# Four column modes per mixing matmul, one save of row modes on ScalarE's queue, way back in two tiles, 15 buffers at once

## The chip, the cores and the metric

The kernel runs on one core of one Trainium2 chip. The metric is the device time of one execution in microseconds (us), from repeated runs; lower is better. Beside it stands one execution that the hardware profiler recorded, with every instruction of the five engines (TensorE, called PE, with its weight loads as PEld; VectorE, DVE; ScalarE, ACT; GpSimd, POOL; SyncE, SP) and every DMA packet.

## What is computed

Two layers on one image x of 512 x 512 positions with 64 channels, all in float32.

```
x  = x + L0(group_norm(x))        # gated products of rows, masked; an output gate
x1 = x
out = x1 + L1(group_norm(x1))
L1: X   = fft2(x1_normed)[:12, :12]              # 12 x 12 modes for each channel
    Y   = einsum("comn,cmn->omn", w_real + 1j*w_imag, X)   # mixes channels, mode by mode
    out = real(ifft2(Y placed at [:12, :12]))
```

The change touches only the second layer, L1, and the end of the first. The group norm is affine for each channel, so its scale enters L1 as a factor on the modes and its shift only in mode (0, 0). The kernel therefore collects modes of x1 while x1 is still being made, and applies the norm afterwards.

## The kernel before, in words

The case with few masked rows (`compact`) is the one that runs. The image is handled in 16 column tiles jc of 32 columns, each in four blocks b of 128 rows; one such tile of 128 rows x 32 columns x 64 channels is 1 MB.

**Main loop (lines 1120 to 1230).** 32 units (half a column tile each, 2 MB) follow one another, each in 8 steps n. The order is written out by hand: each engine takes its instructions in the order of the program (`manual_schedule`). A unit's gate goes PE (L979), DVE (L1194, L1200), ScalarE's sigmoid (L1145), POOL's product and sum (L1038, L1042); the finished x1 is stored by SP to the two halves of a DRAM tensor x1_h (`store`, L1058), and DVE takes group-norm statistics of it (L1096). For each tile, PE collects the row modes in PSUM (`transform`, L1069) and `save` (L1075 to L1090) copies them to SBUF on ScalarE (L1077) and writes them by four DMAs of 48 KB to DRAM, `modes_d`, in runs of 256 bytes. Each group of 128 columns is read back by `fetch` (L904) and turned to column modes by PE (`columns`, L896). The last group has 96 columns, tiles 12 to 14; its fetch is issued by ScalarE, at step 5 of the last unit (L1224). Tile 14 is "the last tile but one", `jc == NJ - 2`. Tile 15's modes do not go through DRAM: they are multiplied at L1083 with a basis that ScalarE prepares at steps 2 to 5 of the last unit (`prepare`, L912, 24 activations).

The mixing weights w_real and w_imag (2.3 MB each) are loaded by SP, two DMAs of 64 partitions x 36 KB, at step 3 of the last unit but one (L1230).

**Between the loops (L1234 to L1287).** POOL clears `picks`. The statistics are joined to the affine `ab2` (`group_norm_affine`, L251 to L277; the matmul L1254 stands inside it). DVE writes the scaled modes to `picks` (L1265): for each row mode m and column mode n a block of 128 x 32 that is zero but for two columns. The mixing (L1275) is 144 matmuls, one for each (m, n): 32 columns of `picks` are stationary, and the 64 columns `wide[:, :, m * MODES + n]` of the weights stream past; twelve of them add up in PSUM for each m, and four m at a time use the four column groups of the array. DVE copies the result to `mixed` (L1284).

**Way back.** `back_columns` is called four times, for 128 columns each, the first time before the last loop: 8 matmuls (L1303), copies to `q` (L1312 on DVE for half of the first call, L1314 on ScalarE for the rest), 16 transposes (L1319), and copies to `parts`, which lies where the weights lay (L1322, L1324).

**Last loop (L1332 to L1356).** For each of the 64 tiles: four matmuls (L1340), four DVE additions to the tile of x1 (L1347), a store of 1 MB by SP (L1348). The tiles of x1 are gathered by rows with indirect DMAs on POOL (`fetch_rows`, L923; the DMA's own line is L629), into a ring of AHEAD = 15 buffers. Buffers 13 and 14 lie in `picks`, so their gathers come after the mixing (L1279).

Of the kernel before, what the change touches and what calls it, by code (L numbers as in the profile page):

```python
# [17 lines left out]
P = 128  # L18
N = 512
C = 64  # L20
# [26 lines left out]
def conv_preact_kernel(ctx: ExitStack, tc: tile.TileContext, t: dict):  # L47
# [565 lines left out]
    def compact(fc):  # L613
# [193 lines left out]
        with tc.tile_pool(name="tri", bufs=1) as trp:  # L807
# [57 lines left out]
            with tc.manual_schedule(), tc.tile_pool(name="late", bufs=1) as lp:  # L865
# [65 lines left out]
                with tc.tile_pool(name="np_x", bufs=LEAD + 2) as tp, tc.tile_pool(  # L931
# [143 lines left out]
                    def save(jc):  # L1075
                        ft = places[:, 7 * 64 * C + M2 * C : 7 * 64 * C + 32 * C].rearrange("p (j c) -> p j c", c=C)
                        nc.scalar.copy(ft.rearrange("p j c -> p (j c)"), fs.pop(jc))  # L1077
                        if jc == NJ - 1:
                            ps = ends[0].rearrange("p m n -> p (m n)")
                            for j in range(8):  # L1080
                                for k in range(2):
                                    e = spread_e[:, j, k].rearrange("p m n -> p (m n)")
                                    nc.tensor.matmul(  # L1083
                                        ps[k * C : (k + 1) * C], ft[:, j, :], e,
                                        start=False, stop=(j == 7), tile_position=(0, k * C),
                                    )
# [33 lines left out]
                    for s in range(-LEAD, total_g + 2 * SIZE):  # L1120
# [110 lines left out]

                with tc.tile_pool(name="lq", bufs=1) as qp, tc.tile_pool(name="lx", bufs=1) as xp:

                    picks = qp.tile([P, MODES, MODES, 32], F32, name="picks")  # L1234
                    fetch_rows(len(fetched))
                    nc.gpsimd.memset(picks, 0.0)
                    buffers += [xp.tile([P, JC, C], F32, name=f"lx_t{i}") for i in range(3)]
                    buffers += [place(i)[:, r * JC : (r + 1) * JC] for i in (0, 1) for r in range(2)]
                    spare = places[:, 7 * 64 * C - 8 * 2 * MODES * M2 : 7 * 64 * C]
                    for spare in (spare, picks.rearrange("p m n k -> p (m n k)")):  # L1240
                        buffers += [spare[:, i * JC * C : (i + 1) * JC * C].rearrange("p (n c) -> p n c", c=C) for i in range(2)]
                    for i in range(len(fetched), AHEAD - 2):
                        fetch_rows(i)
                    rinv = qp.tile([P, 4, P], F32, name="rinv")
                    nc.scalar.dma_start(rinv, t["c_rinv"])
                    col_inv = qp.tile([P, 2, 4, P], F32, name="col_inv")
                    nc.scalar.dma_start(col_inv, t["c_col_inv"])
                    with tc.tile_pool(name="sps", bufs=1, space=PSUM) as sps:

                        turned = sps.tile([P, MODES, M2], F32, name="turned")  # L1250

                        def turn_sums():
                            nc.vector.tensor_add(sums, sums, ends[0])
                            nc.tensor.matmul(  # L1254
                                turned.rearrange("p m n -> p (m n)"), turn, sums.rearrange("p m n -> p (m n)"),
                                start=True, stop=True,
                            )

                        ab2 = group_norm_affine(lp, sets, 8, "x1c", turn_sums)
                        v = qp.tile([P, 2, MODES, MODES], F32, name="v_modes")  # L1260
                        nc.vector.tensor_add(v[:, 0], sums[:, :, :MODES], turned[:, :, MODES:])
                        nc.vector.tensor_sub(v[:, 1], turned[:, :, :MODES], sums[:, :, MODES:])
                        for k in range(2):
                            to = picks.rearrange("p m n k -> p m (n k)")[:, :, 12 * k : 12 * k + 33 * 11 + 1 : 33]
                            nc.vector.tensor_scalar(to, v[:, k], ab2[:, 0:1], None, ALU.mult)  # L1265
                            h = slice(k * C, (k + 1) * C)
                            one = picks[h, 0, 0, 12 * k : 12 * k + 1]
                            nc.vector.scalar_tensor_tensor(one, ab2[h, 1:2], float(N * N), one, ALU.mult, ALU.add)

                        mixed_ps = sps.tile([P, 3, C], F32, name="mixed_ps")  # L1270
                        for m3 in range(3):
                            for n in range(MODES):
                                for g in range(4):
                                    m = 3 * g + m3
                                    nc.tensor.matmul(  # L1275
                                        mixed_ps[32 * g : 32 * g + 32, m3, :], picks[:, m, n, :], wide[:, :, m * MODES + n],
                                        start=(n == 0), stop=(n == MODES - 1), tile_position=(0, 32 * g),
                                    )
# [12 lines left out]
                    q = qp.tile([P, C, 32], F32, name="q_sb")  # L1291
                    nc.vector.memset(q[:, :, M2:], 0.0)

                    def back_columns(jb, pq, pt, first):

                        it = parts[:, jb // 2, : 256 * 16].rearrange("p (j o) -> p j o", o=16)
                        for g2 in range(2):
                            ps = pq.tile([P, 2, 4, 2, C], F32, name="q_ps")[:, :, :3]
                            for part in range(2):
                                for i in range(2):  # L1300
                                    g = 2 * g2 + i
                                    h = slice(32 * g, 32 * g + M2)
                                    nc.tensor.matmul(  # L1303
                                        ps[:, i, :, part, :], col_inv[h, part, jb, :], mixed[h],
                                        start=True, stop=True, tile_position=(32 * g, 0),
                                    )
                            for i in range(2):
                                g = 2 * g2 + i
                                dst = q[:, :, 6 * g : 6 * g + 6].rearrange("p o r -> p r o")
# [5 lines left out]
                        by = q.rearrange("p (o g) r -> p o (g r)", g=4)  # L1315
                        for o4 in range(4):
                            ps = pt.tile([P, 4, P], F32, name="it_ps")
                            for i in range(4):
                                nc.tensor.transpose(ps[:, i, :], by[:, 4 * o4 + i, :], ident)  # L1319
# [48 lines left out]
def _constants():  # L1368
# [19 lines left out]
    for part, rows_ in enumerate(((c.T, -s.T), (s.T, c.T))):  # L1388
# [4 lines left out]
    made = {  # L1393
        "c_last_basis": last_basis.reshape(P, RB, M2),
        "c_last_mask": last_mask,
        "c_col_inv": col_inv.reshape(P, 2, 4, P),
        "c_turn": np.kron([[0, 1], [-1, 0]], np.eye(C)),
        "c_iota": np.tile(np.arange(N), (P, 1)),
# [34 lines left out]
```

## Time and profile before

| | |
|---|---|
| runs of the kernel, median of 3 (lowest to highest) | 1845.44 us (1840.19 to 1845.79) |
| the profiled execution | 1835.84 us |
| its span, first to last instruction | 1834.1 us |
| granted TensorE clock, mean | 0.901 |
| PE, DVE, ACT, POOL busy | 89%, 78%, 52%, 52% |
| DMA, mean over the span | 255 GB/s |
| HBM read, written | 278.05 MB, 187.56 MB |

The profile's page has the busy time of each engine, the span in 40 slices with the granted clock and the DMA rate, the chain of work that ended last, and the costliest groups of instructions. The trace behind it answers further questions: who waited for whom, the chain in order of time, busy time and DMA rate in any stretch, and the DMA packets by queue. q1 is SP's DMA queue, q10 is ScalarE's, q0 POOL's. "issue" is time in which the engine waited for nothing that the profile shows. A name with "q" behind it (ACTq, SPq) is the engine's sequencer.

### The profile page before, as it was taken

What the parts mean: (1) busy time and instruction counts of PE and PEld (TensorE: products, weight loads), DVE (VectorE), ACT (ScalarE), POOL (GpSimd) and SP (SyncE); (2) the same over time, 40 slices, a digit from 0 to 9 for tenths busy, and PEclk for the clock granted to TensorE, in tenths of its full rate; (3) what the DMA queues carried; (4) which work ended last, traced back from release to release, by engine and by line L of the source; (5) the groups of instructions that cost most, each with busy time, mean ns of one, the idle gap of its engine ahead of it and who ended that gap; (6) DMA issues with size and microseconds to landing.
All of it is one profiled execution on the core that took longest, in us unless ns stands there. A gap on an engine that the chain in (4) does not pass through costs nothing.

```text
span 1834.1 us, 33997 instructions
## 1 busy us (share of the span) xinstructions
PE 1628.8 (89%) x11630; PEld 1286.6 (70%) x11630; DVE 1422.9 (78%) x2969; ACT 962.2 (52%) x1694; POOL 947.5 (52%) x709
## 2 busy tenths in 40 slices
PE   6679799999899999999999999999999856998772
PEld 5666666664678778897788888888888734665431
DVE  6989677777455547788999999999999975775442
ACT  3566555554222269976777777777777630111000
POOL 3666211111000007788999999999999881112110
PEclk9989899999899999999999999999999977555555
DMA  6999255556656513577777877776777797999999
GB/s 250 386 385 383 86 138 137 137 137 154 208 178 182 175 34 151 221 241 252 260 247 239 291 261 243 237 266 235 257 261 256 219 297 292 424 427 426 426 427 383
DMA packets 188312, 467.97 MB, mean 255 GB/s; under 512 B 34529, under 2 KB 133857, under 8 KB 147041
## 3 DMA queue, kind: packets, MB, share of 16 engines
q1 hardware_dynamic: 158192, 262.40, 42.5%
q0 software_dynamic: 27712, 201.40, 29.2%
q8 instruction: 95, 1.56, 0.3%
q10 hardware_dynamic: 2224, 1.88, 0.3%
q14 instruction: 89, 0.72, 0.1%
HBM read 278.05 MB, written 187.56 MB: 254 GB/s over the span
## 4 chain that ended last, share of the span: by engine, by line
PE 25%; DVE 18%; DMA 12%; POOL 3%; issue 2%; ACT 2%; SPq 1%; DVEq 0%; ACTq 0%; POOLq 0%
DMA out_x<-places 8%; PE w_ps L979 5%; PE c_ps L979 5%; DVE stats2c L1096 4%; DVE z_t L1194 4%; PE t_ps L969 4%; DVE scratch L1012 4%; PE l_ps L1340 4%; PE y_ps L990 4%; DVE z_t L1200 4%; PE f_ps L1069 2%; DMA modes_d<-places 1%; POOL z_t L1038 1%; POOL places L1042 1%; DMA places<-x_h,dst_i 1%
## 5 line engine op out<-in xcount | busy, mean ns | idle before, releaser
L979 PE MATMUL w_ps<-gate_x,xt_c 128*128 128x128 f32 x2048 | 279.5, 280 | 32.3 <-DVE z_t L1194 30.6
L1042 POOL TENSOR_TENSOR places<-places,z_t 128x1024 f32<-128x1024 f32 x127 | 301.1, 2371 | 8.0
L979 PEld LDWEIGHTS w_ps<-gate_x,xt_c 128*128 128x128 f32 x2048 | 251.0, 193 | 48.0 <-DVE z_t L1194 47.8
L979 PE MATMUL c_ps<-center_x,xt_c 128*128 128x128 f32 x2048 | 276.5, 279 | 1.2 <-ACT xt_c L1008 0.6
L979 PEld LDWEIGHTS c_ps<-center_x,xt_c 128*128 128x128 f32 x2048 | 252.4, 194 | 4.0 <-ACT xt_c L974 2.9
L1096 DVE BATCH_NORM_STATS2 stats2c<-places 128x6 f32<-128x128 f32 x1024 | 220.6, 279 | 12.8 <-POOL places L1042 12.8
L1340 PE MATMUL l_ps<-places,rinv 24*128 24x512 f32 x512 | 204.0, 1106 | 29.3 <-DVE places L1347 18.2
L1012 DVE TENSOR_REDUCE scratch<-sq_c 128x16 f32<-128x1024 f32 x160 | 194.6, 1217 | 27.9 <-ACT sq_c L1007 19.4
L1145 ACT ACTIVATE z_t<-z_t 128x1024 f32<-128x1024 f32 x128 | 135.4, 1059 | 138.0 <-DVE z_t L1200 126.1
L1198 POOL TENSOR_TENSOR z_t<-z_t,bias_row_out 128x1024 f32<-128x1024 f32 x32 | 75.7, 2364 | 245.8 <-DVE z_t L1194 241.7
L969 PE MATMUL t_ps<-c_ident,places 128*128 128x128 f32 x1280 | 198.8, 278 | 1.3 <-DVE places L854 1.3
L1340 PEld LDWEIGHTS l_ps<-places,rinv 24*128 24x128 f32 x512 | 119.4, 298 | 108.6 <-DVE places L1347 57.1
L969 PEld LDWEIGHTS t_ps<-c_ident,places 128*128 128x128 f32 x1280 | 144.4, 141 | 60.3 <-issue 50.9
L974 ACT ACTIVATE xt_c<-t_ps,ab_xc 128x512 f32<-128x512 f32 x256 | 176.2, 688 | 10.3 <-PE t_ps L969 9.3
L1194 DVE TENSOR_TENSOR z_t<-w_ps,rs_n 128x512 f32<-128x512 f32 x256 | 172.1, 672 | 3.0 <-PE w_ps L979 2.9
L1004 ACT ACTIVATE sq_c<-c_ps 128x512 f32<-128x512 f32 x256 | 150.7, 589 | 31.3 <-PE c_ps L979 30.8
L1200 DVE TENSOR_TENSOR z_t<-z_t,scratch 128x1024 f32<-128x1024 f32 x128 | 156.3, 1221 | 10.0 <-ACT rs_n L1018 3.8
L679 DVE BATCH_NORM_STATS2 stats1c<-x_ps 128x6 f32<-128x512 f32 x256 | 156.5, 687 | 8.3 <-PE x_ps L678 7.8
L1038 POOL TENSOR_TENSOR z_t<-z_t,places 128x1024 f32<-128x1024 f32 x64 | 151.6, 2369 | 17.0 <-ACT z_t L1145 13.6
L1347 DVE TENSOR_TENSOR places<-places,l_ps 128x512 f32<-128x512 f32 x176 | 110.2, 684 | 59.3 <-DMA places<-x_h,dst_i 39.8
L1038 POOL TENSOR_TENSOR z_t<-z_t,bias_row_out 128x1024 f32<-128x1024 f32 x63 | 149.3, 2370 | 10.0 <-ACT z_t L1145 9.8
L733 POOL COPY rbc<-rq_out 128x512 f32<-128x512 f32 x64 | 38.3, 613 | 210.5 <-DVE rq_out L209 132.1
(213 smaller groups left out, 2744.3 us busy)
## 6 DMA issues: line engine op xcount, KB each, us to landing
x_h<-places SPq DMA_DIRECT2D x64, 1024.0 KB
out_x<-places SPq DMA_DIRECT2D x44, 1024.0 KB
places<-u_d SPq DMA_DIRECT2D x512, 64.0 KB
left_d<-o_c SPq DMA_DIRECT2D x64, 256.0 KB
right_d<-o_c SPq DMA_DIRECT2D x64, 256.0 KB
left_raw<-left_d SPq DMA_DIRECT2D x64, 256.0 KB
right_raw<-right_d SPq DMA_DIRECT2D x64, 256.0 KB
u_d<-z_t SPq DMA_DIRECT2D x32, 512.0 KB
```

The lines of the kernel that those rows point to most:

```text
L679: nc.vector.bn_stats(stats[:, 0, 16 * (jc % quarter) + 4 * r + c, :], ps.rearrange("p i k -> p (i k)"))
L969: nc.tensor.transpose(tps[:, i, :], flat[:, o : o + P], ident)
L974: nc.scalar.activation(xts[s], tps, AF.Identity, bias=ab1[:, 2:3])
L979: nc.tensor.matmul(ps[:, 2 * i : 2 * i + 2, :], xts[s][:, i, :], w, start=True, stop=True)
L1004: nc.scalar.activation(sq, cps, AF.Square)
L1012: nc.vector.tensor_reduce(totals[k % 2][:, 8 * (n - 1) : 8 * (n + 1)], sqs.pop(s // 2), AX.X, ALU.add)
L1038: nc.gpsimd.tensor_mul(zs[k, c], zs[k, c], u)
L1042: nc.gpsimd.tensor_add(xr, xr, zs.pop((k, c)))
L1096: nc.vector.bn_stats(st[k // 4][:, g, k % 4, :], x_of(k)[:, :, 2 * g : 2 * g + 2])
L1194: nc.vector.tensor_mul(z[:, 8 * odd : 8 * odd + 8, :], wps, rs)
L1200: nc.vector.tensor_add(z, z, bias_ps["ogate"].unsqueeze(1).to_broadcast([P, 16, C]))
L1340: nc.tensor.matmul(ps.rearrange("p j o -> p (j o)"), rinv[h, b, :], it[h], start=True, stop=True, tile_position=(32 * g, 0),)
```

## The change

1. `save` of tile 14 issues its four DMAs to `modes_d` on ScalarE's queue in place of SP's, and the fetch of the last 96 columns is issued at step 4 of the last unit in place of step 5.
2. `picks` holds, for each m, three blocks (q) in place of twelve: a block has the scaled modes of four column modes in four adjacent columns. A matmul of the mixing takes one block against 256 streamed columns (16 x 4 x 4: the 64 channels, reordered, times four n). There are 36 of them, three for each m. Of a row's four sums, one belongs to it: the mask `pick4` (a new constant of 128 x 4, loaded on ScalarE's queue) and a sum over four pick it out. The reordering of the channels that the three copies did is now in the streamed operand. `picks` is a quarter of its size.
3. `q` becomes two tiles of 32 channels. In the first call of `back_columns` DVE copies the first tile and ScalarE the second; in the others ScalarE copies both. The zeros behind them are set by POOL, in place of DVE.
4. The last loop's buffers 4 to 8 are five tiles of a pool (there were three), and none lies in `picks`; all 15 gathers stand before the mixing.

```diff
                         for g in range(4):
                             o = jc * JC + 8 * g
-                            nc.sync.dma_start(modes_d[o : o + 8].rearrange("j m c -> m j c"), ft[32 * g : 32 * g + M2])
+                            queue = nc.scalar if jc == NJ - 2 else nc.sync
+                            queue.dma_start(modes_d[o : o + 8].rearrange("j m c -> m j c"), ft[32 * g : 32 * g + M2])
...
-                        if (v, n) == (last, 5):
+                        if (v, n) == (last, 4):
                             fetch(3)
...
-                    picks = qp.tile([P, MODES, MODES, 32], F32, name="picks")
+                    picks = qp.tile([P, MODES, 3, 32], F32, name="picks")
...
-                    buffers += [xp.tile([P, JC, C], F32, name=f"lx_t{i}") for i in range(3)]
+                    buffers += [xp.tile([P, JC, C], F32, name=f"lx_t{i}") for i in range(5)]
...
-                    for i in range(len(fetched), AHEAD - 2):
+                    for i in range(len(fetched), AHEAD):
                         fetch_rows(i)
+                    pick4 = qp.tile([P, 4], F32, name="pick4")
+                    nc.scalar.dma_start(pick4, t["c_pick4"])
...
                         for k in range(2):
-                            to = picks.rearrange("p m n k -> p m (n k)")[:, :, 12 * k : 12 * k + 33 * 11 + 1 : 33]
-                            nc.vector.tensor_scalar(to, v[:, k], ab2[:, 0:1], None, ALU.mult)
+                            for q in range(3):
+                                nc.vector.tensor_scalar(
+                                    picks[:, :, q, 12 * k + 4 * q : 12 * k + 4 * q + 4], v[:, k, :, 4 * q : 4 * q + 4],
+                                    ab2[:, 0:1], None, ALU.mult,
+                                )
...
-                        mixed_ps = sps.tile([P, 3, C], F32, name="mixed_ps")
+                        mixed_ps = sps.tile([P, 3, C, 4], F32, name="mixed_ps")
+                        by_mode = wide.rearrange("p (g o) a -> p o g a", g=4)
                         for m3 in range(3):
-                            for n in range(MODES):
+                            for q in range(3):
                                 for g in range(4):
...
                                     nc.tensor.matmul(
-                                        mixed_ps[32 * g : 32 * g + 32, m3, :], picks[:, m, n, :], wide[:, :, m * MODES + n],
-                                        start=(n == 0), stop=(n == MODES - 1), tile_position=(0, 32 * g),
+                                        mixed_ps[32 * g : 32 * g + 32, m3].rearrange("p (o g) r -> p o g r", g=4),
+                                        picks[:, m, q, :], by_mode[:, :, :, m * MODES + 4 * q : m * MODES + 4 * q + 4],
+                                        start=(q == 0), stop=(q == 2), tile_position=(0, 32 * g),
                                     )
-                        for i in range(AHEAD - 2, AHEAD):
-                            fetch_rows(i)
...
+                        nc.vector.tensor_mul(
+                            own, mixed_ps.rearrange("p m c r -> p (m c) r"), pick4.unsqueeze(1).to_broadcast([P, 3 * C, 4])
+                        )
                         mixed = qp.tile([P, 3, C], F32, name="mixed")
-                        for m3 in range(3):
-                            nc.vector.tensor_copy(
-                                mixed[:, m3, :].rearrange("p (o g) -> p g o", g=4),
-                                mixed_ps[:, m3, :].rearrange("p (g o) -> p g o", g=4),
-                            )
+                        nc.vector.tensor_reduce(mixed.rearrange("p m c -> p (m c)"), own, AX.X, ALU.add)
...
-                    q = qp.tile([P, C, 32], F32, name="q_sb")
-                    nc.vector.memset(q[:, :, M2:], 0.0)
+                    qs = [qp.tile([P, C // 2, 32], F32, name=f"q_sb{i}") for i in range(2)]
+                    for q in qs:
+                        nc.gpsimd.memset(q[:, :, M2:], 0.0)
...
-                                if first and i == 0:
-                                    nc.vector.tensor_copy(dst, src)
-                                else:
-                                    nc.scalar.copy(dst, src)
+                                for k, q in enumerate(qs):
+                                    dst = q[:, :, 6 * g : 6 * g + 6].rearrange("p o r -> p r o")
+                                    o = k * C // 2
+                                    if first and k == 0:
+                                        nc.vector.tensor_copy(dst, src[:, :, o : o + C // 2])
+                                    else:
+                                        nc.scalar.copy(dst, src[:, :, o : o + C // 2])
```

`own` lies in the first 768 elements of each partition of `picks`. As built, the engines keep their order otherwise. One wait comes with the new queue: DMAs share eight completion semaphores in turn, and a DMA waits for the one before it on its semaphore. w_imag's load on SP now follows, on its semaphore, the first of the four writes on ScalarE's queue, and waits for its landing; before, it followed an older load.

More of the change, by code (lines that the diff above doesn't have):

```diff
@@ L1232, in compact @@
                 with tc.tile_pool(name="lq", bufs=1) as qp, tc.tile_pool(name="lx", bufs=1) as xp:
-                    picks = qp.tile([P, MODES, MODES, 32], F32, name="picks")
+                    picks = qp.tile([P, MODES, 3, 32], F32, name="picks")
                     fetch_rows(len(fetched))
                     nc.gpsimd.memset(picks, 0.0)
-                    buffers += [xp.tile([P, JC, C], F32, name=f"lx_t{i}") for i in range(3)]
+                    buffers += [xp.tile([P, JC, C], F32, name=f"lx_t{i}") for i in range(5)]
                     buffers += [place(i)[:, r * JC : (r + 1) * JC] for i in (0, 1) for r in range(2)]
                     spare = places[:, 7 * 64 * C - 8 * 2 * MODES * M2 : 7 * 64 * C]
-                    for spare in (spare, picks.rearrange("p m n k -> p (m n k)")):
-                        buffers += [spare[:, i * JC * C : (i + 1) * JC * C].rearrange("p (n c) -> p n c", c=C) for i in range(2)]
-                    for i in range(len(fetched), AHEAD - 2):
+                    buffers += [spare[:, i * JC * C : (i + 1) * JC * C].rearrange("p (n c) -> p n c", c=C) for i in range(2)]
+                    for i in range(len(fetched), AHEAD):
                         fetch_rows(i)
+                    pick4 = qp.tile([P, 4], F32, name="pick4")
+                    nc.scalar.dma_start(pick4, t["c_pick4"])
                     rinv = qp.tile([P, 4, P], F32, name="rinv")
@@ L1268, in compact @@
                             nc.vector.scalar_tensor_tensor(one, ab2[h, 1:2], float(N * N), one, ALU.mult, ALU.add)
-                        mixed_ps = sps.tile([P, 3, C], F32, name="mixed_ps")
+                        mixed_ps = sps.tile([P, 3, C, 4], F32, name="mixed_ps")
+                        by_mode = wide.rearrange("p (g o) a -> p o g a", g=4)
                         for m3 in range(3):
-                            for n in range(MODES):
+                            for q in range(3):
                                 for g in range(4):
-                                    m = 3 * g + m3
+                                    m = MODES // 4 * g + m3
@@ new lines, in compact @@
+                                        picks[:, m, q, :], by_mode[:, :, :, m * MODES + 4 * q : m * MODES + 4 * q + 4],
+                                        start=(q == 0), stop=(q == 2), tile_position=(0, 32 * g),
+                                    )
+                        own = picks.rearrange("p m q k -> p (m q k)")[:, : 3 * C * 4].rearrange("p (c r) -> p c r", r=4)
+                        nc.vector.tensor_mul(
+                            own, mixed_ps.rearrange("p m c r -> p (m c) r"), pick4.unsqueeze(1).to_broadcast([P, 3 * C, 4])
+                        )
@@ L1308, in back_columns @@
                                 g = 2 * g2 + i
-                                dst = q[:, :, 6 * g : 6 * g + 6].rearrange("p o r -> p r o")
                                 src = ps[:, i].rearrange("p m k o -> p (m k) o")
-                                if first and i == 0:
-                                    nc.vector.tensor_copy(dst, src)
-                                else:
-                                    nc.scalar.copy(dst, src)
-                        by = q.rearrange("p (o g) r -> p o (g r)", g=4)
+                                for k, q in enumerate(qs):
[5 more added lines that the diff above has]
+                                        nc.scalar.copy(dst, src[:, :, o : o + C // 2])
                         for o4 in range(4):
@@ L1318, in back_columns @@
                             for i in range(4):
-                                nc.tensor.transpose(ps[:, i, :], by[:, 4 * o4 + i, :], ident)
+                                by = qs[o4 // 2].rearrange("p (o g) r -> p o (g r)", g=4)
+                                nc.tensor.transpose(ps[:, i, :], by[:, 4 * (o4 % 2) + i, :], ident)
                             dst = it[:, (jb % 2) * P : (jb % 2 + 1) * P, 4 * o4 : 4 * o4 + 4].rearrange("p j o -> p o j")
@@ L1395, in _constants @@
         "c_last_mask": last_mask,
+        "c_pick4": (np.arange(P) % 32 % MODES % 4)[:, None] == np.arange(4)[None, :],
         "c_col_inv": col_inv.reshape(P, 2, 4, P),
```

## Prediction

> **What bounds the kernel now.** I read the page's slices first: the change touches only work after 1455 us, so I cut that part with the windows view (columns: stretch, us, then busy time of PE, PEld, DVE, ACT, POOL, then granted clock, DMA share, GB/s).
>
> ```profile
> 1462.00:1488.00 26.00, 15.72 (x97) 11.34 (x96) 23.43 (x64) 16.53 (x33) 24.68 (x12) 0.93 0.94 201
> 1488.00:1531.00 43.00, 21.65 (x338) 16.15 (x338) 21.04 (x83) 3.15 (x5) 19.30 (x14) 0.68 1.00 396
> 1531.00:1560.00 29.00, 19.96 (x117) 14.17 (x108) 17.28 (x28) 4.82 (x6) 3.74 (x4) 0.65 0.60 219
> 1560.00:1820.00 260.00, 206.56 (x560) 125.52 (x560) 147.03 (x236) 18.64 (x23) 44.01 (x47) 0.51 1.01 426
> ```
>
> From 1560 us to the end the DMA engines are full at 426 GB/s: 64 MB of output and 49 MB of gathers, 118.5 million bytes, take 278 us. So the end hangs on when the first output store can start (1547.83 us on SP, L1348); from it to the end are 286.3 us. Before it, in 1531 to 1560 us, the DMA engines run at half that rate. The chain in order of time (start, us, what) says what holds the store back:
>
> ```profile
> 1465.89 26.98 DMA modes_d<-places
> ...
> 1493.05 7.57 DMA places<-modes_d
> ...
> 1500.66 5.31 PE t_ps L896 x24
> 1505.98 3.35 PE f_ps L1069 x16
> ...
> 1510.04 4.10 PE t_ps L1083 x32
> ...
> 1521.38 3.97 PE mixed_ps L1275 x121
> 1525.35 2.11 issue
> 1527.46 3.76 PE mixed_ps L1275 x121
> 1531.22 2.72 issue
> 1533.94 1.11 PE mixed_ps L1275 x26
> ```
>
> Four 48 KB writes take 27 us, a read-back 7.6 us, and the mixing 13.7 us, 4.8 of them in gaps. The waits add that ScalarE stands in line for the writes, with the last unit's sigmoids behind the fetch:
>
> ```profile
> ACT z_t L1145 <- DMA modes_d<-places: 6.8, 1, 6.8
> ```
>
> **The row modes on ScalarE's queue.** Why 27 us? On SP's queue the writes stand behind both mixing weights, 128 packets of 36,864 bytes. The trace's packets show eight rounds of these, from 1461.4 to 1488.4 us, some 2.6 us each. Other queues do not stand behind them; they take turns. The DMA view, first for 1469 to 1486 us (weights, 16 completions; gather), then for 1488 to 1490.5 us (writes of 256 bytes; gather), has columns packets, MB, share:
>
> ```profile
> q1 hardware_dynamic: 96, 2.95, 78.6%
> q0 software_dynamic: 96, 0.79, 22.0%
> ```
> ```profile
> q0 software_dynamic: 108, 0.83, 88.7%
> q1 hardware_dynamic: 117, 0.10, 13.1%
> ```
>
> One packet for one packet, whatever their sizes. The writes are 768 packets of 256 bytes, 48 on each of 16 engines.
>
> ScalarE issues them after L1077, at 1464.7 us; four issues at 0.39 us (L1090's median) fit the 2.01 us in which it then waits for DVE. If that cover went, 1.6 us would be added to a sigmoid. ScalarE's queue needs 3.4 us to its first packet (fetch 1493.05 to 1496.47, rinv 1509.48 to 1512.94), so they start at 1468. As built, w_imag's load waits for the first of them; until it lands only w_real is ahead, four rounds, done by about 1472.6. Two or three small packets pass each engine by then; the rest alternate with the gather's six remaining packets at 0.33 us, then run alone at 0.02 us: the first write lands at about 1475, all by 1476.5 (before: 1492.87). Behind the waiting w_imag on SP stand only x1 stores, which were behind the weights anyway. w_imag then runs from 1477.5, four rounds of 2.6 to 3.4 us, to 1488 to 1491 (before 1488.4); the mixing needs it 25 us later.
>
> The fetch, a step earlier, stands behind 18 of the 24 L912: ScalarE reaches it at 1482.39 + 4.25/2 = 1484.5 us (twelve L912 took 4.25) and finds its data there. Six more L912 follow, then the sigmoid at 1487.0 instead of 1493.4. The one behind it waits for DVE (1489.4) and starts at 1489.5 instead of 1494.5, so the last unit is complete 4.9 us earlier. The fetch has six packets of 6 KB per engine: one or two turns beside w_imag, the rest with stores and gather at 0.31 + 0.31 + 0.23 us, so it lands at about 1495 (before 1500.62): 5.2 us earlier, within 3 and 8. PE's chain behind it (L896, L1069, L1083) is still later than the statistics on DVE, which shift by 4.9 and had 2 us to spare. Term: **-5.2 us**; from -8 to 0.
>
> [...]
>
> **The mixing.** 36 matmuls x 2 passes in four column groups are 18 rounds of 256 streamed columns; before, 72 rounds of 64: the same 4608. Before, a pair of weight load and matmul took 30 ns in both bursts (3.97/132, 3.76/128) although the granted clock rose from 0.50 to 0.92: bound by instructions. L1069's rounds of 512 columns show streaming: 0.86 us at the low clock (1505.91, 1506.77, 1507.62), about 0.43 at the full one (two rounds in 1.07 us with the tail). So a round of 256 takes 0.43 or 0.215 us. The stage began at 0.50 and was faster after about 4 us: 9 rounds at 0.43, 9 at 0.215, 5.9 us. Ends: 3.9 (all at full clock) and 8.5 (the old rate per column, 0.118/64) plus one gap of 2.4, 10.9. The gaps come every 264 instructions or so; now there are 144. Value 5.9: **-7.8 us**, from -9.8 to -2.8.
>
> Added on the path: six L1265 of 48 elements at the 0.19 us of other small DVE rows, against two of 0.35: +0.5. After it, a product of 768 from PSUM (L1194: 512 in 0.67, L1200: 1024 in 1.22, so 0.95) and a sum of 768 (L1012: 1024 in 1.22; L1113: 256 in 0.51; so 0.98), against 0.53 for three copies: +1.4. Together **+1.9**, from 1.4 to 2.5. POOL's clearing shrinks from 3.96 to about 1 us and only lets it wait sooner.
>
> **Way back.** Before, DVE and ScalarE copied to one tile, and ScalarE's first copy waited for DVE's: 1537.10 to 1539.38, 2.3 us for four. Now four halves run on each at once; a half of 0.80 to 0.81 is 0.4 at least, 0.5 with fixed cost: 1.6 to 2.0, and transposes of the first half start before. **-0.4**, from -0.7 to 0. POOL's two clearings stand behind eleven gathers at 1.24 us, done by about 1516, ten us ahead of need. In the three later calls ScalarE has eight halves for four copies of 0.82: up to +0.8 us each, under a full DMA; without that cover 2.4 us.
>
> **Buffers.** The two late gathers (issued 1535.55 and 1536.79) had landed by 1543, ahead of the store. Moved up, they fill 4.9 us of idle DMA. Worth 0 alone, but the earlier store needs it: from about 1489, four stores, twelve gathers, fetch and constants, 19 million bytes, take 44.7 us at 425 GB/s, to 1534. The store would be at 1547.8 - 11.5 = 1536.3: DMA is no bound until the chain gains some 14 us.
>
> **Sum.** -5.2 - 7.8 + 1.9 - 0.4 = -11.5 us against the profiled execution, 1835.84 us (span 1834.1): 1824.3, with a span of 1822.6. That execution is 0.52% below the runs' median, so in runs: 1845.44 x 1824.3/1835.84 = **1834 us**, 0.62% faster. About 0.3% (5.5 us) is what a measurement of this kernel can tell from no change.
>
> **Rivals.**
> - [...] -6.3 us, 1839. Chance 0.17.
> - *The mixing streams slowly* (low clock throughout, or a gap stays): 8.5 to 10.9 us. For it: PE is idle 3.6 us ahead of it and its clock had fallen to 0.50. Against it: fewer, longer instructions. -6.5 to -9, about 1837. Chance 0.15.
> - *ScalarE waits longer, slower*: it takes its instructions in order, and now six L912 (2.1 us) and both sigmoids stand behind the fetch. If the writes met 8 KB packets of both other queues in all 48 turns (0.64 us each), they would land at 1469.7 + 31 = 1501, the sigmoids 10 us late, 2 of them covered, +8 - 6.3: 1847. It loses from a landing at about 1499 on, and by over 0.3% from 1505. Against it: one gather has 8 packets per engine, and SP's stores wait behind w_imag. Chance 0.06.
> - *DMA fills first* (gathers start late or w_imag's delay pushes stores): -3 to -5, 1841. Against it: 44.7 us fit. Chance 0.06.
>
> Forecast: 0.56. Left ends: first term -8 and mixing at full clock, -14 where DMA binds; 1831, less 3 for the spread of runs. Slow mixing, slow queue: 1839 to 1842. Range 1828 to 1842; the forecast's own 1831 to 1837. Faster by over 0.3%: 0.56 + 0.10 + 0.10 = 0.76; within 0.3%: 0.18; slower: 0.06.
>
> **What would show it.** w_imag's issue at about 1476 on SP; L904 at about 1485 on ScalarE with hardly a wait; its data at 1493 to 1497; the mixing in 5 to 7 us without gaps over 1 us; the first store at about 1536; 1531 to 1560 us well over 219 GB/s. Wrong: a wait of ScalarE for modes_d that is still over 5 us, or a mixing over 8.

## The result, and the profile after

| | median (runs) | kernel before, run beside it | ratio, 95% interval |
|---|---|---|---|
| after | 1838.03 us (10) | 1843.16 us (10) | 0.9964, 0.9949 to 0.9979 |
| after, a second time | 1831.01 us (11) | 1838.81 us (32) | 0.9960, 0.9947 to 0.9973 |

The ratio is worked out from all runs of a pair, so it is not quite that of the two medians. By it the change is worth 6.6 to 7.4 us, where 11.5 were forecast. Lines behind 1090 have moved: the mixing is L1282 (was L1275), the way back's copies L1320 and L1322, the last loop's matmuls L1348.

The same stretches as before, then the chain in order of time and the waits, all of the changed kernel:

```profile
1462.00:1488.00 26.00, 18.01 (x113) 12.71 (x113) 23.41 (x64) 14.89 (x28) 24.63 (x12) 0.93 0.93 227
1488.00:1531.00 43.00, 22.35 (x126) 14.22 (x130) 25.01 (x97) 5.49 (x12) 22.67 (x20) 0.58 0.96 344
1531.00:1560.00 29.00, 22.05 (x118) 15.17 (x110) 16.81 (x26) 3.81 (x6) 1.88 (x2) 0.56 0.76 302
1560.00:1820.00 260.00, 210.73 (x565) 126.74 (x561) 148.78 (x239) 20.02 (x36) 44.01 (x47) 0.51 1.01 424
```
```profile
1485.32 16.11 DMA places<-modes_d
...
1501.48 5.31 PE t_ps L896 x24
1506.80 3.67 PE f_ps L1069 x16
...
1511.12 6.37 PE t_ps L1083 x32
1517.49 0.60 PE mean_ps L253 x2
...
1526.97 6.96 PE mixed_ps L1282 x72
1533.93 2.07 issue
```
```profile
POOL lx_t L629 <- DVE part L251: 13.3, 1, 13.3
...
PE t_ps L896 <- DMA places<-modes_d: 11.9, 1, 11.9
...
DVE mean L255 <- PE mean_ps L253: 5.3, 1, 5.3
...
ACT z_t L1146 <- DVE z_t L1201: 2.8, 2, 1.9
```

The 27 us of `modes_d` writes have left the chain, and ScalarE's 6.8 us wait for them is gone. But the fetch, issued 7.7 us sooner on the trace's time (11.5 us sooner counted from w_real's issue), takes 16.1 us where it took 7.6; PE waits for it, and DVE with the finished statistics waits for `mean_ps`, which stands behind L896, L1069 and L1083 in PE's order. The mixing is one piece of 7.0 us where there were three with gaps, and there is a new wait of POOL.

Yet these two profiles show no gain: from w_real's issue to the end are 375.84 us before and 375.75 after. The profiled execution of before (1835.84 us) was faster than all ten of its timed runs; that of after (1839.54 us) was the slowest of its ten. One pair of profiles can't carry a difference of 0.4%, so both kernels were profiled again. The table gives the steps in us from the issue of tile 14's first row-mode write. "Last statistics" is the end of DVE's last L1097 (L1096 before). "Part 1" and "part 2" are the first two points of the change, each without the others; the last three columns are the experiments one_q, modes_first and early, further down.

| | before | before, again | after | after, again | part 1 alone | part 2 alone | one q | modes first | both early |
|---|---|---|---|---|---|---|---|---|---|
| columns start (L896) | 36.0 | 36.3 | 33.1 | 32.6 | 32.3 | 35.6 | 33.3 | 32.5 | 21.9 |
| last statistics (DVE) | 41.0 | 41.4 | 36.1 | 36.1 | 36.1 | 40.8 | 36.1 | 36.1 | 36.1 |
| f_ps ends (L1069) | 44.6 | 45.2 | 42.0 | 41.4 | 41.2 | 44.4 | 42.1 | 41.4 | 30.9 |
| L1083 ends | 49.5 | 50.1 | 49.1 | 48.1 | 48.0 | 51.2 | 49.3 | 48.1 | 35.9 |
| mixing starts | 56.7 | 57.6 | 58.6 | 55.7 | 55.2 | 58.7 | 56.8 | 55.7 | 47.6 |
| mixing takes | 13.6 | 13.1 | 6.9 | 5.9 | 13.3 | 6.1 | 6.2 | 5.9 | 5.6 |
| first store | 83.2 | 84.8 | 81.5 | 77.0 | 81.2 | 78.3 | 76.6 | 77.0 | 68.7 |
| from it to the end | 286.2 | 286.2 | 287.8 | 286.9 | 287.6 | 287.6 | 287.6 | 287.9 | 289.5 |

### The profile page after: what moved, and what is told of

Read it like the earlier page. It is cut to its first block, busy times and chain, and to the rows that moved or that the text cites. A ratio compares the mean times of both kernels' runs of the same rounds, so it can differ in the third digit from the quotient of the medians.

```text
span 1837.7 us, 33577 instructions
## 1 busy us (share of the span) xinstructions
PE 1637.7 (89%) x11414; PEld 1287.7 (70%) x11414; DVE 1423.6 (77%) x2973; ACT 961.9 (52%) x1708; POOL 945.3 (51%) x711
## 4 chain that ended last, share of the span: by engine, by line
PE 29%; DVE 16%; DMA 9%; POOL 4%; issue 3%; ACT 1%; DVEq 0%; POOLq 0%; ACTq 0%
PE c_ps L979 6%; PE w_ps L979 6%; PE t_ps L969 5%; PE l_ps L1348 4%; DVE stats2c L1097 4%; DMA places<-x_h,dst_i 4%; PE y_ps L990 4%; DVE z_t L1195 3%; DVE scratch L1012 3%; DVE z_t L1201 3%; PE f_ps L1069 2%; POOL z_t L1038 2%; DMA out_x<-places 2%; POOL places L1042 2%; DMA lx_t<-x_h,dst_i 2%
## 5 line engine op out<-in xcount | busy, mean ns | idle before, releaser
L1348 PE MATMUL l_ps<-places,rinv 24*128 24x512 f32 x512 | 207.8, 1124 | 29.3 <-DVE places L1355 18.6
L1097 DVE BATCH_NORM_STATS2 stats2c<-places 128x6 f32<-128x128 f32 x1024 | 220.5, 278 | 12.5 <-POOL places L1042 12.5
L1348 PEld LDWEIGHTS l_ps<-places,rinv 24*128 24x128 f32 x512 | 120.3, 303 | 111.9 <-DVE places L1355 59.6
L1004 ACT ACTIVATE sq_c<-c_ps 128x512 f32<-128x512 f32 x256 | 150.5, 588 | 30.9 <-PE c_ps L979 29.4
L1038 POOL TENSOR_TENSOR z_t<-z_t,places 128x1024 f32<-128x1024 f32 x64 | 151.6, 2369 | 16.2 <-ACT z_t L1146 13.3
```

Of the source, the lines that this page charges most:

```text
L1004: nc.scalar.activation(sq, cps, AF.Square)
L1038: nc.gpsimd.tensor_mul(zs[k, c], zs[k, c], u)
L1097: nc.vector.bn_stats(st[k // 4][:, g, k % 4, :], x_of(k)[:, :, 2 * g : 2 * g + 2])
L1348: nc.tensor.matmul(ps.rearrange("p j o -> p (j o)"), rinv[h, b, :], it[h], start=True, stop=True, tile_position=(32 * g, 0),)
```

## The experiments

My theory after these two profiles: the mixing gave what was forecast; of the row modes' gain, the half is lost because the fetch lands late, so that PE's chain and not the sigmoids' is the path. The rival: position is worth nothing, and both halves of the forecast were too large.

**Both kernels again.** No edit.

> The kernel before, unchanged. Both theories: a ratio of 1.000 within 0.002. It is run for its profile. The profiled execution of before (1835.84 us) was below all ten of its timed runs, that of after (1839.54 us) was the slowest of its ten, so the two traces, whose stretches from w_real's issue to the end are 375.84 and 375.75 us, show no difference where the timed runs show 6.6 us. Theory A (the profile of before was an outlier in its own tail): this one has the matmuls of L1083 at 6 us and more instead of 4.10, and a stretch of 378 us or more from w_real's issue to the end. Rival B (the profile was ordinary in the tail and the extra time of the timed runs lies ahead of 1458 us): L1083 again near 4.1 us, the stretch 375 to 377 us, and w_real's issue later than 1458.

> The changed kernel, unchanged. Ratio 0.996 (0.994 to 0.998). Theory A (the profiled run of after was a slow one of its kind, with a TensorE clock of 0.50 in 1510 to 1515 us): this profile ends 4 to 6 us earlier, L1083 takes nearer to 4.1 us than 6.4, and the stretch from w_real's issue to the end is 370 to 373 us. Rival B (the tail of after is what the trace showed): the stretch is again 375 to 376 us and any difference lies ahead of w_real's issue. In either case POOL's first gather into lx_t waits some 13 us and w_imag's issue is held some 20 us on SP's queue.

Measured: before 0.9997 (0.9985 to 1.0009), after 0.9960. In between: L1083 of before took 4.10 us again, so that theory A fell there, but its stretch from w_real's issue was 377.43 us, 1.6 longer. After's second profile has a stretch of 370.36 us, 5.4 less than its first, as its theory A had it; but L1083 stays near 6 us, and not near 4.1. In the table the first store comes 4.5 us earlier. The mixing is 1 us shorter, and in the first profile DVE stood still for 1.8 us ahead of its last write to `picks`, for which the mixing waits; the second has no such pause. The lines are the pause in the first profile, then two of the second's chain:

```profile
DVE picks L1273 <- DVE picks L1267: 1.8, 1, 1.8
```
```profile
1511.25 5.88 PE t_ps L1083 x32
...
1524.73 5.95 PE mixed_ps L1282 x72
```

Why DVE paused is not known. From the second pair, 377.4 to 370.4, the profiles say 7.1 us, as the runs do; from the first they say 0.1. So one pair can be off by some 7 us, and it is the runs that give the gain.

**The first part alone** (the kernel before, with the queue of `save` and the step of the fetch as in the change).

```diff
+                            queue = nc.scalar if jc == NJ - 2 else nc.sync
...
-                        if (v, n) == (last, 5):
+                        if (v, n) == (last, 4):
```

> The kernel before with the first part alone: the last modes write but one on ScalarE's queue, the fetch one step earlier. My prediction priced it at -5.2 us: ratio 0.997, 1838 us. Theory A (the part is worth what the sigmoids gain, and the fetch that lands 16 us after its issue eats the rest): last sigmoid 4.9 us earlier against w_real's issue, columns 2.9 earlier, and all of the 2.9 reaches the end: -2 to -4 us, ratio 0.998. Rival B (position is worth nothing because the fetch shares the engines with w_imag's 36 KB packets): columns no earlier, ratio 1.000.

Measured: 0.9985 (0.9970 to 0.9999), -2.8 us. The last sigmoid, and with it the statistics, come 4.9 to 5.3 us earlier, the columns 3.7 to 4.0, the mixing 1.5 to 2.4.

```profile
1484.87 15.33 DMA places<-modes_d
...
1509.88 6.03 PE t_ps L1083 x32
```

The fetch takes twice its 7.6 us, and L1083, at 6.03 us, 1.9 more than before's 4.10 (the clock, below). Rival B falls, as the columns do come earlier. Theory A's time fits, but not all of the columns' gain reaches the mixing: L1083 takes back the difference.

**The second part alone** (four column modes to a matmul; `few` is a view of the first quarter of the old `picks`, so no buffer moves).

```diff
+ held_all = picks.rearrange("p m n k -> p (m n k)")
+ few = held_all[:, : 3 * MODES * 32].rearrange("p (m q k) -> p m q k", m=MODES, k=32)
...
+                                        few[:, m, q, :], by_mode[:, :, :, m * MODES + 4 * q : m * MODES + 4 * q + 4],
```

> The kernel before with the second part alone: four column modes to a matmul with the mask product and the sum, the small picks as a view of the first 1152 elements of the old large tile, so that no buffer moves and two gathers still wait for the reduce. Predicted -5.9 us (-7.8 for the matmuls, +1.9 for the product, the sum and the six L1265): ratio 0.9968. Theory A (mixing is 7.0 us long where 13.6 were, the other terms as predicted): -4.5 to -5 us, ratio 0.9975, and the first store 4 to 5 us earlier. Rival B (a DVE wait of 1.8 us and 2 us more ahead of PE's first mixing matmul are caused by the mixing's own code): -1 to -2 us, ratio 0.999.

Measured: 0.9969 (0.9956 to 0.9983), -5.7 us; -5.9 was predicted, and theory A's -4.5 to -5 lies inside the interval. The chain has the old writes and the new mixing:

```profile
1467.33 26.75 DMA modes_d<-places
...
1524.83 6.09 PE mixed_ps L1284 x72
```

The two parts alone multiply to 0.9954, -8.5 us; the whole is 0.996. Within these intervals nothing large is hidden in their meeting.

**The new wait of POOL.** v_modes and mixed laid in the ring's place for the modes:

```diff
-                        v = qp.tile([P, 2, MODES, MODES], F32, name="v_modes")
+                        free_t = modes_t.rearrange("p m c -> p (m c)")
+                        v = free_t[:, : 2 * MODES * MODES].rearrange("p (k m n) -> p k m n", k=2, m=MODES)
```

> The changed kernel with v_modes and mixed laid into the modes' region of the ring, which is free by then, so that the pool behind them begins 1,920 bytes lower and the last of the five lx buffers ends at byte 222,624, below the statistics (222,848), where after's ended at 224,544. Theory A (that overlap of 1,696 bytes is why POOL's first lx gather waited 13.26 us in after): the gather is issued some 42 to 44 us behind w_real's issue (after 51.2 and 50.6, before 46.4 and 46.7), and 1488 to 1531 us carries near 400 GB/s (after 344). On the time, theory A1 (the first store is set by the chain of PE, DVE and ScalarE, and the gathers have landed by then in either kernel): first store and total as after, ratio 0.996 within 0.0015. Theory A2 (the gathers' lateness is where the missing 3 us went, by DMA queues that begin the way back with less done): ratio 0.994. Rival B (the wait is for the statistics themselves, wherever the buffers lie): gather again at 50 us and more.

Measured: 0.9958 (0.9945 to 0.9971). The cause is shown: with the two tiles out of the pool the last of the five buffers no longer reaches into the place of the statistics, and the first lx gather goes out 38.1 us behind w_real's issue instead of 50.6 to 51.2 (42 to 44 expected). And so is its price, none that can be measured: the DMA rate recovers, the first store does not move (78.3 us on the table's scale, after 77.0 and 81.5).

```profile
1488.00:1531.00 43.00, 24.08 (x166) 14.68 (x166) 23.47 (x89) 2.35 (x5) 18.52 (x18) 0.64 0.97 393
```

**One q tile as before.**

```diff
-                    qs = [qp.tile([P, C // 2, 32], F32, name=f"q_sb{i}") for i in range(2)]
+                    q = qp.tile([P, C, 32], F32, name="q_sb")
```

> The changed kernel with the way back as before: one q tile, DVE and ScalarE each copying one whole group. The prediction priced the halves at -0.4 us. Theory A (the halves read one PSUM tile in turns, each engine waiting 0.55 us for the other, so that q_ps to l_ps took 9.32 and 8.70 us in after against 8.45 and 8.78 in before): q_ps to l_ps 8.4 to 8.8 us, ratio equal to after's 0.996 or up to 0.0005 lower. Rival B (the prediction): ratio 0.0002 higher, that is not to be told apart in the time, and q_ps to l_ps 0.4 us longer than after's on average.

Measured: 0.9958 (0.9945 to 0.9971), the same as after. From the first q_ps to the first it_ps are 3.37 us; after's second profile has 3.95. The DVE timeline of that one, then of this kernel (start, us, what, idle before and its releaser):

```profile
1534.73 0.80 DVE L1320 COPY q_sb<-q_ps 128x192 f32<-128x192 f32 x2 [0.55 <-ACT q_sb L1322]
```
```profile
1532.06 1.44 DVE L1317 COPY q_sb<-q_ps 128x384 f32<-128x384 f32 x2 [1.06 <-PE q_ps L1308]
```

With halves, DVE and ScalarE read one PSUM tile and take turns, each waiting 0.55 us for the other's copy; the trace shows a wait for a semaphore, and what sets it was not tested. They do not run side by side: the eight halves take 3.4 us from the first's start to the last's end, the four whole copies 2.3. From q_ps to l_ps are 7.8 us, less than the 8.4 expected; after's second profile has 8.7. So in this pair the part costs 0.6 to 0.9 us. Over all profiles the steps from q_ps to it_ps overlap (halves 3.95 to 4.68 in six, one tile 3.29 to 4.16 in eight), and in the time nothing shows.

**Why the fetch lands late.** First smaller weight packets, then another order.

```diff
-                                nc.sync.dma_start(wide[part * C : (part + 1) * C], t[name].rearrange("c o m n -> c o (m n)"))
+                                for o in range(0, C, 16):
+                                    nc.sync.dma_start(
+                                        wide[part * C : (part + 1) * C, o : o + 16],
+                                        t[name].rearrange("c o m n -> c o (m n)")[:, o : o + 16],
+                                    )
```

> The changed kernel with each of the two weight loads in four, so that their packets are 9 KB and not 36 KB. Theory A (after's fetch takes 16 us from issue to landing because its 6 KB packets alternate one for one with w_imag's 36 KB packets of 2.5 to 3.0 us): the fetch lands 8 to 11 us after its issue and columns start at 32 to 35 us behind w_real's issue (after 39.5 and 39.0); the last sigmoid stays at 31.3; the total gains 1 to 2 us more, ratio 0.9952, as f_ps and L1083 follow the columns by 9 and 15 us until the statistics (42.5) bind. Rival B (it is the amount of bytes in flight and not the packet's size): landing 14 us or more after the issue, ratio 0.996.

```diff
-                            queue = nc.scalar if jc == NJ - 2 else nc.sync
+                            queue = nc.sync
...
-                        if (v, n) == (last, 4):
+                        if (v, n) == (last, 0):
...
-                        if v == last - 1 and n == 3:
+                        if v == last - 1 and n == 5:
```

> The changed kernel with the modes writes back on SP's queue but the weight loads issued behind them, and the fetch at step 0 of the last unit. Theory A (the part is worth what the fetch's landing and the sigmoids gain, whichever queue; the queue's 3.4 us to the first packet and w_imag's hold of 20 us on SP were its price): modes written within 8 us of their issue, no wait of ScalarE, columns at the latest 35 us behind the same point of the chain (load of unit 31) where after's were 39; the end 1 to 2 us earlier than after, ratio 0.9952. Rival B (the weights, issued 7 us later, land too late for the mixing): PE waits for them at the first mixing matmul, ratio 0.997 to 1.000. Rival C (columns are no bound any more once the fetch lands at 39): no change, 0.996.

Measured: 0.9966 (0.9953 to 0.9980) and 0.9956 (0.9944 to 0.9969). Neither is better than after. In w_pieces the fetch took 12.9 us to the columns, not the 8 to 11 expected, and the last sigmoid came 1.4 us later, as ScalarE's four issues of the writes took 3.3 us instead of 1.8. Its first store is at 75.4 us, 1.6 ahead of after's second profile, but from there to the end are 289.2. In modes_first the writes landed 2.7 us after their issue and the fetch went out 10 us earlier in the chain, and still the columns waited for it:

```profile
PE t_ps L896 <- DMA places<-modes_d: 10.8, 1, 10.8
```

The trace's packets say why. The fetch's 96 packets (six per engine) took, from first to last:

| | first packet after the issue | first to last | weight packets meanwhile |
|---|---|---|---|
| before | 3.4 us | 3.5 us | none |
| after, again | 7.3 us | 7.1 us | 36 KB, for half of it |
| modes first | 7.4 us | 17.5 us | 36 KB throughout |
| both (next) | 6.5 us | 7.1 us | 9 KB throughout |

With weights in flight, the first packet came 3.1 to 4.0 us later than in before, beside 36 KB and 9 KB packets alike; from the first packet to the last it took 17.5 us beside 36 KB and 7.1 beside 9 KB, in two kernels that differ in nothing else.

**Both**: the edits of the last two together.

> The changed kernel with both: modes writes on SP's queue ahead of the weight loads, the weights in pieces of 9 KB, the fetch at step 0 of the last unit. In modes_first the fetch was issued 11.9 us sooner against w_real's own stretch but landed 26 us later, in w_pieces it was issued late but landed in 12.9. Theory A (from the last sigmoids on, f_ps ends 8.6 to 8.9 us behind the start of the columns in every kernel, so the columns and with them the fetch's landing have been the path, and packets of 36 KB are what holds the fetch): columns no longer wait for the DMA, start at 28 us or less behind the issue of the modes writes (after 33.1 and 32.6, before 36.0 and 36.3), f_ps ends at 39 us or less (after 42.0 and 41.4), the first store 2 to 3 us earlier, ratio 0.9945. Rival B (the statistics take over at once): f_ps at 41 us, ratio 0.996. Rival C (the path gains 2 to 3 us, but the stretch from the first store to the end grows by as much): first store earlier and ratio 0.996.

Measured: 0.9927 (0.9911 to 0.9943), 1826.67 us, -13.4 us against before, more than any of the theories had. The columns start at 21.9 us on the table's scale and L1083 is done at 35.9, as the statistics end; now PE waits for DVE at `mean_ps`, where DVE had waited for PE:

```profile
PE mean_ps L253 <- DVE part L251: 3.9, 1, 3.9
```

The mixing starts 8 us earlier than in after's second profile, 1.7 of them by a shorter L1083 (4.2 us for 5.9). That is what the late fetch still cost there, with the slower L1083 that goes with it. And the DMA engines are full from 1488 us on, at a share of 1.01:

```profile
1488.00:1531.00 43.00, 26.02 (x189) 16.98 (x188) 28.05 (x98) 6.58 (x11) 19.73 (x18) 0.70 1.01 373
1531.00:1560.00 29.00, 24.40 (x89) 16.54 (x86) 17.20 (x28) 6.64 (x12) 4.17 (x5) 0.56 1.01 425
```

So of 8.3 us at the first store (77.0 to 68.7) 2.6 are given back behind it (286.9 to 289.5): what is not moved by then has to be moved later.

**One gather more ahead.** One q, laid into the ring, and a sixteenth buffer in its room:

```diff
-AHEAD = 15
+AHEAD = 16
...
+                    q = place(7)[:, :JC].rearrange("p n c -> p (n c)").rearrange("p (o r) -> p o r", r=32)
```

> The changed kernel with one q tile as before, laid into the modes' and ft's place of the ring, v_modes and mixed into the rest of spread_e's, and a sixteenth buffer in the room that this frees, so that one gather more goes out ahead of the first store. Theory A (from the first store to the end the DMA engines are full, 423 to 426 GB/s and share 1.01, while ahead of it they stand idle for some 7 us: what counts is how much is moved by then): first store as in one_q, the stretch from it to the end 2.4 us shorter (1 MB at 424 GB/s; 287.6 to 285.2), ratio 0.9945. Rival B (the end is set by the chain of adds and back_columns, not by bytes): the stretch stays at 287 to 288 us, ratio 0.996.

> Both of the two kernels above in one. If both theories A hold, 2 to 3 us of the one and 2.4 us of the other, less what the gathers lose by a first store that comes earlier: ratio 0.993 to 0.994. If only one holds, 0.9945 to 0.995. If neither, 0.996.

Measured: 0.9942 (0.9927 to 0.9956), and with "both" 0.9926 (0.9911 to 0.9940). Alone it gains, by one profile each: first store at 76.4 us as in one q, 284.2 us from there to the end instead of 287.6; in the runs the intervals of the two overlap. With "both" it adds nothing. The stretch behind the first store is 2.6 us shorter than in "both" (287.0), but the first store comes 2.8 us later (71.5): the first q_ps starts 4.8 us behind the mixing, where 2.1 are usual, as it waits for the constant `col_inv`, a DMA of 512 KB on ScalarE's queue that took 19.2 us to land beside full DMA engines (a share of 1.01 from 1488 us on). There was little idle DMA time left to fill, and a load that the path needs came late once more; what an earlier load of `col_inv` would give was not tried.

**The weights' rate.** Does a load in pieces move faster than 9 KB in 0.7 us when the two weights come on two queues? As early_sixteen, with w_imag on ScalarE's queue behind the fetch:

```diff
+ for part, at in enumerate(((last - 1, 5), (last, 1))):
+     if (v, n) == at:
+         queue, name = ((nc.sync, "w_real"), (nc.scalar, "w_imag"))[part]
```

> early_sixteen with w_imag on ScalarE's queue, in two pieces behind the fetch, while w_real stays in four on SP's. In early and early_sixteen the DMA engines are full from 1488 us to the end, so that they and no longer the chain set the time, and the weight packets move 9 KB in 0.67 to 0.76 us where the gathers' 8 KB take 0.31. [...] Rival B (the rate is that of the source or of the packet's kind, whichever partitions it goes to): packets stay at 0.7 us, ratio 0.9925, as early_sixteen. Rival C (ScalarE is held by the two issues, and the last sigmoid comes later than 24.8 us behind the modes writes): slower than early_sixteen.

Measured: 0.9925 (0.9912 to 0.9938), no change. It does not decide: w_real's last packet ended at 1489.02 us and w_imag's first one began at 1489.12, so the two never ran side by side. So rival B's ratio was met without a test of its cause, and why the weights move at half the gathers' rate (211 GB/s for 423, below) stays open. Rival C fell: the last sigmoid came at 24.8 us. From the first write to the end this profile has 355.9 us, "both" 358.2; the runs don't show that difference.

## Why the prediction was right or wrong

Direction and the main mechanisms were right, the size was not: 6.6 to 7.4 us instead of 11.5. The 1838 us lie in the range given, but above the forecast's own 1831 to 1837. That the second session's 1831.01 falls into that band is luck: the kernel before ran at 1838.81 there, 4.4 us lower than in the first.

1. **Row modes, forecast -5.2, measured -2.8** (alone, 0.2 to 5.5 by the interval). This is the step that failed. Its first half held in time: writes all landed 13.1 us after their issue (forecast 11.8, before 27.8), ScalarE did not wait, the last unit came 4.9 to 5.3 us earlier. But it did not come about as forecast. The writes' first packet came 8.1 us after their issue (forecast 3.4), in w_real's last round, so that they passed next to nothing of w_real. What they escaped was w_imag, and that because the shared semaphore held its issue back until the first write had landed. Had its four rounds of 2.9 us been in flight, the writes would have landed at some 13.1 + 11.6 = 24.7 us, an estimate that no run tried. The failing sentence is "The fetch has six packets of 6 KB per engine: one or two turns beside w_imag, the rest with stores and gather at 0.31 + 0.31 + 0.23 us, so it lands at about 1495". The fetch was even issued 2.9 us sooner than forecast (23.4 us behind w_real's issue for 26.3), but it took 15.6 to 16.1 us to land where 10.5 were forecast. I took the first packet at 3.4 us behind the issue, the row of an idle queue; it took 6.3 to 7.4. And w_imag, so held back, was issued 19.4 to 19.6 us behind w_real (forecast 17.8) and ran until 34 to 35 us behind it (forecast 30 to 33), into the fetch. From w_real's issue the data was due at 36.8 us; the columns started at 39.0 to 39.5. That the PE chain was later than the statistics I had said, and it is why only the columns' gain counts: 3.3 us between the means of the two pairs. In "both" the same sigmoids with an early fetch bring the mixing 8 us forward against after's second profile.
2. **A term that was missing: L1083 at the low clock.** I carried its 4.10 us over. It is 5.9 to 6.6 us in eight of the profiles with a change, +1.8 to +2.5, between in one (5.5), and 4.1 to 4.2 in three; it goes with the clock, below. In part 1 alone it is already in the -2.8 us.
3. **Mixing, forecast -7.8: measured -6.5 and -7.5** (13.4 us, the mean of before's two profiles, to 6.9 and 5.9 in after's two). In all eleven profiles that have it, it takes 5.6 to 6.9 us; forecast 5.9. The rival that it streams slowly, 8.5 us and more, is refuted.
4. **Product and sum, +1.4: +1.4** (from the last mixing matmul to q_ps 2.11 us, before 0.71). The six small DVE writes: at most +0.4 (7.5 to 7.6 us from L1083 to the mixing, before 7.2 and 7.5; after's first profile has 9.5, with the pause of DVE), forecast +0.5.
5. **Way back, -0.4: about +0.6**, by one pair of profiles and not to be told in the runs. "Now four halves run on each at once" was wrong; they alternate.
6. **Buffers, 0: right for after**, though POOL's first lx gather came to wait 13 us, which the trace of before could not show, since it comes of where the last of five buffers lies. That wait was free too. "DMA is no bound until the chain gains some 14 us" held: "both" gained 15.3 us at the first store and found the engines full (1531 to 1560 us at 425 GB/s). What the forecast missed is the other side of it: a gather more ahead is worth 3.4 us, by one pair of profiles, as long as they are not.
7. **From the first store to the end**, 286.2 us in both profiles of before, 286.9 to 288.0 in the seven that have neither weight pieces nor a sixteenth buffer. Some 1.4 us are given back there. I can't explain it: either part alone has it too, at 287.6, without moving a buffer.

The rival of -6.3 us, the sum without the first term, was that the writes' position in a queue is worth nothing. It is refuted as a mechanism: the same 768 small packets were written 27.8 us after their issue behind the weights and 2.7 at the head of the same queue. The 13.1 us on ScalarE's queue don't decide it, as w_imag was held back there. But the packets of different queues do interleave: the fetch's six per engine took 17.5 us among w_imag's and w_real's in modes first. In size, too, the rival came nearer than the forecast: -6.3 us, where 6.6 to 7.4 were measured, and 1839 us against 1838.03.

## What to carry to other kernels

Moving a small transfer to another queue frees it from what stands ahead of it on the old one, not from what flies beside it (here the writes landed 13.1 us after their issue for 27.8, and the fetch took 15.6 to 16.1 us for 7.6): look whether the big load is really in flight at that time, or held back by a wait, and price the reader behind it with the packet sizes of the other queues, or cut the big load into small packets and issue it later (the fetch's packets took 7.1 us beside 9 KB, 17.5 beside 36 KB). When a wait is removed, look at the next one in the same engine's order (here PE's: fetch, columns, f_ps, L1083, then the statistics' matmul); a gain upstream that this order does not let through is worth only its slack. For changes under 1%, take two profiles of each kernel before reading a difference.

## What the runs showed of the hardware

**The granted clock changed on a grid.** In the traces of before and after every stretch of one clock, but for the last that the trace's end cuts off, lasts a multiple of 3.41 us (6.83, 10.24, 20.48, ...). So does, by windows of 1 us, every whole stretch around L1083 (1494 to 1552 us) in eight more profiles; the grid's phase differs from run to run. In before and after the clock falls to 0.50 at 1488.3 and 1488.4 us, for 20.5 and 27.3 us. In these ten profiles it comes back 2.9 to 4.3 us after f_ps starts in the two of before and in w_pieces, but 8.0 to 9.3 us in the seven others. f_ps lasts 3.3 to 3.7 us. In the first three it fills 79 to 85% of the step of the grid that ends as the clock rises; in the seven it fills at most 74% of any step, and the clock rises only behind a later one, in L1083. In three of the seven (after, lx_moved, one q) L896's matmuls alone fill a whole step ahead of f_ps, and the clock does not rise. L1083 takes 4.10 us in before, where all of it runs at 1.00, and 5.9 to 6.4 in after's two profiles, the two parts alone and modes first. What sets the moment of the rise was not tested.

**The weights' load to 64 partitions ran at about half the gathers' rate**: 36,864 bytes in 2.67 us per engine, 16 engines, are 221 GB/s, in pieces of 9 KB 0.70 us each, 211; the gathers' 8 KB in 0.31 us are 423. The cause was not tested. It is not a fixed rate of the load: in split16 w_imag's packets of 18 KB, in turns with 8 KB packets of stores and gathers, took 1.05 us, 281 GB/s, while those took 0.4 to 0.6 us instead of 0.31.

**A queue's first packet** came 0.8 us after the issue for the writes at the head of SP's queue and 3.4 us for before's fetch on ScalarE's. With weights in flight at the issue, it came 6.3 to 7.4 us behind the issue for the fetch and 5.0 to 8.1 us behind it for the writes on ScalarE's queue.
